# Eight gated blocks on one core: maxima without a clamp, a shared PSUM bank, one copy per mixture tile, and other orders

## The chip, the core and the metric

The kernel runs on one core of a Trainium2 chip. The core has five engines that work through their own lists in order and wait for each other by semaphores: TensorE (PE, with its weight loads PEld), VectorE (DVE), ScalarE (ACT), GpSimd (POOL) and SyncE (SP), which here only issues DMAs. TensorE writes to PSUM alone: 8 banks of 512 float32 per partition. The metric is the device time of one execution in microseconds; the time of a kernel is the median of its runs.

## The reference

`x` is (16, 112, 256), the context (16, 375, 256). Four layers follow each other, each an attention over the context and a feed-forward part, both gated:

```python
x = x + tanh(g_xattn[0]) * L0_xattn(layernorm(x), ctx, ...)          # 16 heads of 16
x = x + tanh(g_ffn[0])   * L0_ffn(layernorm(x), ...)                 # 8 experts, top 2
x = x + tanh(g_xattn[1]) * L1_xattn(layernorm(x), ctx, ctx, mask, ...)
x = x + tanh(g_ffn[1])   * L1_ffn(layernorm(x), ...)                 # 8 experts, top 2
x = x + tanh(g_xattn[2]) * L2_xattn(ctx, ctx, layernorm(x), ...)
x = x + tanh(g_ffn[2])   * L2_ffn(layernorm(x), ...)                 # tokens split over experts
x = x + tanh(g_xattn[3]) * L3_xattn(layernorm(x), ctx, ctx, mask, ...)  # one head
x = x + tanh(g_ffn[3])   * L3_ffn(layernorm(x), ...)                 # products of FP4-rounded values
```

The attention of layer 1 clips and masks its scores:

```python
scores = clip(q @ k.T * scale, -100.0, 100.0)
scores = where(mask == 0, -inf, scores)
out = softmax(scores) @ v
```

A mixture picks two of eight experts per token:

```python
expert_out = einsum('bsd,edo->bseo', x, expert_w) + expert_b
out = sum over the two chosen experts of gate * expert_out
```

## The kernel before

The 16 sequences (`b`) form four groups (`g`) of four; `x` stays in SBUF. The order of the work on PE, ACT, DVE and POOL is the order of the Python code: inside `tc.manual_schedule` nothing is reordered, so each engine meets its instructions as the lines are run.

**PSUM.** `wide` tiles (two banks each, three of them) and `bank` tiles (one bank, two of them) fill it. A new tile of a kind reuses an old one of that kind, and the first writer waits until the old one's readers are done.

**Layers 0 and 2** (`unmasked`) run per sequence: scores for the maxima (`maxima`, four steps `cp`, two wide tiles each, reduced on DVE, L455), the maxima split into three bf16 parts and transposed (`max_parts`, `max_rows`), transposed scores with the maximum subtracted by a small product (`exponentials`, L490 and L502, two wide tiles, ACT's exponential L511), the product with the values (`weighted`, L526, into the bank `po`), `normalised` on DVE, and `output` (L563). Keys of the sequence after next (`both_keys`, wide), values of the next (`values_of`, single banks) and the queries of the next group stand between.

**Layer 1** (`with_mask`) runs in 64 units, four per sequence. A unit issues the scores of the unit ahead (`masked_scores`: PE L439, then on DVE one operation that applies -100 and the upper bound with the mask, L589), transposes the exponentials of its own unit in two halves (`turned`, L623, copied by ACT or DVE, L627), multiplies those of the unit before with the values (`weighted_masked`, L640, into `po`), then `unit_rest`, and `masked_weights` of the unit ahead: DVE's maximum per half (L606), POOL's clamp of it to at most 100 (L608), ACT's four exponentials with their sums (L611). The inverse sums are spread on POOL (`one_over`, L655), transposed into a bank `pr` (`one_over_T`, L663), copied by ACT (L665); `normalised_masked` multiplies `po` with them on DVE, POOL adds a bias (`plus_bv`), and `output` multiplies with `wo` into a bank `py`, which ACT scales (L569) and POOL adds to `x` (L570). `mask_of` makes the upper bound on POOL (L580, L581).

**Mixtures.** `fill()`, called between the steps of the attention, advances three generators by one step each: `route` (norm, logits, top two, places in a table, indirect copies of the rows to DRAM), `products` (14 slots of 128 rows of one expert per group: L1127 and L1137 on PE, L1139 on ACT, L1142 on DVE, then a store) and `combine` (indirect gathers, L1157, and two additions each, L1165). A slot's product lies in one half of a wide tile, and the transposed rows of the next slot in the other half; ACT copies the rows, DVE adds the expert's bias, which a DMA has broadcast to 128 partitions. Group 0 of layer 0 begins to route at sequence 5 of layer 0; groups 2 and 3 are worked off in layer 1, those of layer 1 from its fifth sequence on into layer 2.

Of the kernel before, what the change touches and what calls it, by code (L numbers as in the profile page):

```python
# [25 lines left out]
E = 8  # L26
FF = 1024
FI = 704
P = 128
# [18 lines left out]
def tile_gated_xattn_stack(ctx: ExitStack, tc: tile.TileContext, a: dict, out: bass.AP):  # L48
# [4 lines left out]
    moe = ctx.enter_context(tc.tile_pool(name="moe", bufs=2))  # L53
# [18 lines left out]
    ctxT = [ctxp.tile([P, 2, T], F32, tag=f"ctx{b}", name=f"ctx{b}") for b in range(B)]  # L72
# [4 lines left out]
    def load_ctx(b):  # L77
        nc.sync.dma_start(ctxT[b], a["ctx"][:, :, b * T : (b + 1) * T])
# [38 lines left out]
    slot_rows = ramp(1, NS, P, "slot_rows")  # L117
    coef = const.tile([E, 2], F32, tag="coef", name="coef")
# [109 lines left out]
    def project(ps, w, c, rhs, n):  # L228

        for k in range(2):  # L230
            nc.tensor.matmul(  # L231
                ps[:, :n], w[:, k, c * P : (c + 1) * P], rhs[:, k, :], start=(k == 0), stop=(k == 1)
            )
# [22 lines left out]
    def attention(pool, layer, w):  # L256
# [7 lines left out]
        masked = layer == 1  # L264
        more = {}
# [81 lines left out]
        def keys_of(b, c):  # L347
            if b >= B:
                return
            if c == 0:  # L350
                kTs[b] = pool.tile([P, 2, T], F32, tag="kT", name=f"kT_{L}_{b}", bufs=3)
            pk = bank(f"pk_{L}_{b}_{c}")
            project(pk, w["wk"], c, rhs_of(b), T)
            if "bk" in w:
                nc.scalar.activation(kTs[b][:, c, :], pk[:, :T], AF.Identity, bias=w["bk"][:, c : c + 1])
            else:
                nc.scalar.copy(kTs[b][:, c, :], pk[:, :T])

        def both_keys(b):
            if b >= B:  # L360
                return
            kT = kTs[b] = pool.tile([P, 2, T], F32, tag="kT", name=f"kT_{L}_{b}", bufs=3)
            pk = wide(f"pk_{L}_{b}")
            for c in range(2):
                project(pk[:, c, :], w["wk"], c, rhs_of(b), T)
            if "bk" in w:
                for c in range(2):
                    nc.scalar.activation(kT[:, c, :], pk[:, c, :T], AF.Identity, bias=w["bk"][:, c : c + 1])
            else:
                nc.scalar.copy(kT, pk[:, :, :T])  # L370
# [58 lines left out]
        def scores(b, cp):  # L429
# [4 lines left out]
            for h in range(2):  # L434
                ps = wide(f"ps_{L}_{b}_{cp}_{h}")
                for i in range(2):
# [3 lines left out]
                        ps[:S, i, :T],  # L440
                        qms[g][rows, c, p, j * S : (j + 1) * S],
                        kTs[b][rows, c, :],
# [113 lines left out]
        def output(b):  # L556
# [4 lines left out]
            py = bank(f"py_{L}_{b}")  # L561
            for c in range(2):
                nc.tensor.matmul(py[:S, :D], oT[:, c, :], w["wo"][:, c, :], start=(c == 0), stop=(c == 1))  # L563
            if not masked:
                xb = x[g][:, j, :]
                nc.vector.scalar_tensor_tensor(xb, py[:S, :D], gate[:S, layer : layer + 1], xb, ALU.mult, ALU.add)
                return
            y = pool.tile([S, D], F32, tag="y", name=f"y_{L}_{b}", bufs=1)
# [4 lines left out]
        def mask_of(b):  # L573
# [5 lines left out]
            uppers[b] = pool.tile([S, T], F32, tag="upper", name=f"up_{L}_{b}")  # L579
            nc.gpsimd.tensor_scalar(uppers[b], mk, 0, -BIG, ALU.is_equal, ALU.mult)  # L580
            nc.gpsimd.tensor_scalar(uppers[b], uppers[b], 100.0, None, ALU.add)  # L581
            rss[b] = small.tile([S, H], F32, tag="rs", name=f"rs_{L}_{b}")

        def masked_scores(b, cp):
            if b >= B:
                return
            sm = exs[b, cp] = pool.tile([S, 4, T], F32, tag="ex", name=f"sm_{L}_{b}_{cp}", bufs=4)
            for h, ps in enumerate(scores(b, cp)):
                nc.vector.scalar_tensor_tensor(  # L589
                    sm[:, 2 * h : 2 * h + 2, :],  # L590
                    ps[:S, :, :T],
                    -100.0,
                    uppers[b][:, None, :].to_broadcast([S, 2, T]),
# [4 lines left out]
        def masked_weights(b, cp):  # L598
# [5 lines left out]
            for h in range(2):  # L604
                part = nmax[:, 2 * h : 2 * h + 2]
                nc.vector.tensor_reduce(part, sm[:, 2 * h : 2 * h + 2, :], AX.X, ALU.max, negate=True)  # L606

                nc.gpsimd.tensor_scalar(part, part, 100.0, None, ALU.min)  # L608
                for i in range(2 * h, 2 * h + 2):
                    head = 8 * c + 2 * i + p  # L610
                    nc.scalar.activation(  # L611
                        sm[:, i, :], sm[:, i, :], AF.Exp, bias=nmax[:, i : i + 1], accum_out=rss[b][:, head : head + 1]
# [18 lines left out]
        def weighted_masked(b, cp):  # L631
# [3 lines left out]
            if cp == 0:  # L635
                pos[b] = bank(f"po_{L}_{b}")
# [20 lines left out]
        def one_over_T(b):  # L657
            if b < 0:
                return
            rxf = rss.pop((b, "x")).rearrange("s h d -> s (h d)")  # L660
            pr = bank(f"pr_{L}_{b}")
# [27 lines left out]
        def unmasked(nxt, block):  # L689
# [12 lines left out]
            for b in range(B):  # L702
# [53 lines left out]
                fill()  # L756
                maxima(b + 2, 0)
                weighted(b, 1)
# [5 lines left out]
                values_of(b + 1, (2,))()  # L764
                if at == 1:
                    both_queries(g)
                maxima(b + 2, 1)
                fill()
# [10 lines left out]
        def unit_rest(b, cp, nxt):  # L779
# [3 lines left out]
            if cp == 0:  # L783
                one_over_T(b - 1)
                later.append(values_of(b + 1, (0, 1)))
            elif cp == 1:
                output(b - 1)
# [5 lines left out]
            if at == 3 and cp in (0, 1):  # L793
                queries_T(g, cp)
            elif at == 3 and cp == 2:
                for c in range(2):
                    queries(g, c)
            return later

        def with_mask(nxt):  # L800
# [8 lines left out]
            for u, (b, cp) in enumerate(units):  # L809
# [7 lines left out]
                fill()  # L817
                turned(b, cp, 0)
                if u:
                    weighted_masked(*units[u - 1])  # L820
                if cp % 2:
# [10 lines left out]
                elif cp == 3:  # L832
                    one_over(b)
# [15 lines left out]
            output(B - 1)  # L849
# [63 lines left out]
    )  # L913
    gate_weights = {}
# [9 lines left out]
    def mixture_weights(layer):  # L924
        L = f"L{layer}_ffn_"
        gate_weights[layer] = load(wpool, L + "gate_w", [P, 2, E], "gw"), load_row(L + "gate_b", "gb", E)

    def route(layer, g, out):
# [23 lines left out]
        xT = act.tile([P, 2, GS], F32, tag="xT", name=f"xT_{nm}")  # L952
        for k in range(2):
            pt = bank(f"pt_{nm}_{k}")
            for j in range(G):
                nc.tensor.transpose(pt[:, j * S : (j + 1) * S], xn[:, j, k * P : (k + 1) * P], ident[:S, :S])
            nc.scalar.copy(xT[:, k, :], pt[:, :GS])
            yield
        pl = bank(f"pl_{nm}")
# [46 lines left out]
        yield  # L1006


        pp = bank(f"pp_{nm}")
# [50 lines left out]
        pe = bank(f"pends_{nm}")  # L1060
# [6 lines left out]
        copy_out(0, 0)  # L1067
        yield
        pt = bank(f"ptab_{nm}")
# [8 lines left out]
        copy_out(0, 1)  # L1078
        yield
        for j in range(1, G):  # L1080
            for i in range(2):
                copy_out(j, i)
                yield

    def products(layer, g, routed):
# [13 lines left out]
        def weights_of(s):  # L1099
# [3 lines left out]
            w = ws[s] = moe.tile([P, 3 * D], F32, tag="w", name=f"w_{nm}_{s}", bufs=WB)  # L1103
            nc.sync.dma_start(
# [709 lines left out]
```

## Time and profile before

Nine runs: median 1622.64 us, 1616.84 to 1628.10. The profiled execution took 1616.01 us; its span, from the first instruction to the last, is 1614.2 us, at a mean granted TensorE clock of 0.973.

Stages of the span, busy us of each engine in them (all from the trace; "PE stands" is the length less PE's busy time):

| stage | us | length | PE | PE stands | DVE | ACT | POOL | clock |
|---|---|---|---|---|---|---|---|---|
| start | 0 to 23 | 23.0 | 13.1 | 9.9 | 2.1 | 4.2 | 12.0 | 0.90 |
| layer 0 attention, first mixtures | 23 to 393 | 370.0 | 340.1 | 29.9 | 223.6 | 150.8 | 89.7 | 0.95 |
| layer 1, masked attention, mixtures | 393 to 892 | 499.0 | 431.3 | 67.7 | 357.5 | 281.5 | 225.0 | 0.97 |
| layer 2 attention, last mixtures | 892 to 1250 | 358.0 | 339.9 | 18.1 | 207.6 | 159.2 | 93.6 | 0.99 |
| expert block of layer 2 | 1250 to 1370 | 120.0 | 116.6 | 3.4 | 49.6 | 42.9 | 46.1 | 1.00 |
| last layer | 1370 to 1614.2 | 244.2 | 223.2 | 21.0 | 164.5 | 112.2 | 84.0 | 0.99 |

A busy time counts an engine's instructions, not its waits for them; matmuls overlap, so PE's busy time is an upper bound of its work. The costliest groups that the change touches: L439 PE 1536 records of 531 ns; L589 DVE 128 of 929 ns; L606 DVE 128 of 923 ns; L611 ACT 256 of 600 ns; L608 POOL 128 of 221 ns; L1127 PE 448 of 403 ns; L1139 ACT 104 of 366 ns; L1142 DVE 112 of 423 ns. Views of waits name who waited, then (after the arrow) what ended the wait; a timeline shows the start, the length, the engine, the line and the shape, and in brackets how long the engine had stood before.

### The profile page before, as it was taken

How to read it: one execution, taken by the hardware profiler on the slowest of the kernel's cores; microseconds unless marked ns; L12 is line 12 of the kernel's file. 1: busy time of each engine (PE TensorE's matmuls, PEld its weight loads, DVE VectorE, ACT ScalarE, POOL GpSimd, SP SyncE). 2: the span in 40 equal slices, each digit the busy share in tenths (PEclk: the TensorE clock that was granted, in tenths of full speed). 3: DMA queues.
4: the chain of work that ended last, by engine and by line, in shares of the span. 5: the costliest groups of instructions: out<-in, count | busy, mean ns of one | idle time of the engine just before them, and what ended most of it. 6: DMA issues, size and time to landing. Idle time of an engine off the chain costs nothing.

```text
span 1614.2 us, 34976 instructions
## 1 busy us (share of the span) xinstructions
PE 1464.2 (91%) x13404; PEld 1015.7 (63%) x13404; DVE 1004.9 (62%) x1965; ACT 750.8 (47%) x1550; POOL 550.5 (34%) x1067
## 2 busy tenths in 40 slices
PE   6989899999888798897896899999999999899997
PEld 3555556666666566575674566666666888667765
DVE  2556555676767586777677365656566434476875
ACT  1444334344545555665654344444445333455532
POOL 3212122243444426427317214223212343242342
PEclk8889999999999999999998899999999999999999
DMA  8671014344434243441441242531002551100000
GB/s 245 212 258 49 2 36 120 117 124 108 121 109 127 86 131 108 123 121 60 125 126 56 81 115 71 156 104 32 8 2 86 164 176 49 38 16 19 16 9 18
DMA packets 127262, 150.37 MB, mean 93 GB/s; under 512 B 13496, under 2 KB 118328, under 8 KB 125048
## 3 DMA queue, kind: packets, MB, share of 16 engines
q1 hardware_dynamic: 120520, 133.45, 27.6%
q0 software_dynamic: 6144, 14.69, 3.1%
q8 instruction: 106, 1.74, 0.4%
q14 instruction: 60, 0.49, 0.1%
q10 hardware_dynamic: 432, 0.01, 0.0%
HBM read 103.80 MB, written 44.30 MB: 92 GB/s over the span
## 4 chain that ended last, share of the span: by engine, by line
PE 69%; DVE 14%; ACT 9%; POOL 3%; issue 3%; DMA 1%; SPq 0%; POOLq 0%; ACTq 0%; DVEq 0%
PE pv L406 8%; PE ps L439 8%; PE pk L231 7%; PE pm_m L1127 6%; PE pt L490 5%; PE po L526 4%; PE pe L623 4%; PE py_f L1285 3%; PE ph L1269 3%; PE py L563 3%; PE pq L231 3%; PE pgu_h L1615 2%; DVE nm L455 2%; ACT sm L611 2%; PE py L1649 2%
## 5 line engine op out<-in xcount | busy, mean ns | idle before, releaser
L455 DVE TENSOR_REDUCE nm<-ps 112x2 f32<-112x750 f32 x256 | 228.0, 932 | 188.6 <-PE ps L439 188.2
L439 PE MATMUL ps<-kT,qm 32*112 32x375 f32 x1536 | 196.4, 531 | 19.2 <-ACT kT L370 7.7
L511 ACT ACTIVATE ex<-pt 125x896 f32<-125x896 f32 x192 | 165.6, 914 | 68.9 <-PE pt L502 68.0
L611 ACT ACTIVATE sm<-sm,nmax 112x375 f32<-112x375 f32 x256 | 152.4, 600 | 27.0 <-POOL nmax L608 27.0
L589 DVE SCALAR_TENSOR_TENSOR sm<-ps,up 112x750 f32<-112x750 f32 x128 | 113.5, 929 | 64.5 <-PE ps L439 60.8
L623 PE MATMUL pe<-ident,sm 112*125 112x112 f32 x768 | 118.1, 287 | 37.4 <-ACT sm L611 30.6
L623 PEld LDWEIGHTS pe<-ident,sm 112*125 112x125 f32 x768 | 104.3, 196 | 68.8 <-ACT sm L611 58.2
L1127 PE MATMUL pm_m<-w_m,xgT_m 128*128 128x256 f32 x448 | 125.8, 403 | 7.6 <-DVE nm L455 4.8
L439 PEld LDWEIGHTS ps<-kT,qm 32*112 32x112 f32 x1536 | 66.5, 173 | 79.5 <-issue 27.1
L406 PE MATMUL pv<-w_L_xattn_wv,ctx 128*125 128x256 f32 x384 | 101.1, 401 | 16.0 <-ACT y L569 7.9
L606 DVE TENSOR_REDUCE nmax<-sm 112x2 f32<-112x750 f32 x128 | 112.9, 923 | 0.0
L490 PE MATMUL pt<-qm,kT 32*125 32x224 f32 x1536 | 109.3, 379 | 1.1 <-DVE nm L455 0.7
L1127 PEld LDWEIGHTS pm_m<-w_m,xgT_m 128*128 128x128 f32 x448 | 76.8, 190 | 43.7 <-ACT eT L627 14.9
L1142 DVE TENSOR_TENSOR y_m<-pm_m,w_m 128x256 f32<-128x256 f32 x112 | 47.3, 423 | 84.9 <-ACT xgT_m L1139 78.8
L627 ACT COPY eT<-pe 125x672 f32<-125x672 f32 x96 | 68.8, 717 | 62.2 <-PE pe L623 59.8
L231 PE MATMUL pk<-ctx,w_L_xattn_wk 128*128 128x375 f32 x256 | 93.5, 498 | 1.8 <-ACT qm L392 0.9
L526 PE MATMUL po<-ex,vpad 125*32 125x112 f32 x3072 | 94.6, 263 | 0.3 <-ACT ex L511 0.3
L406 PEld LDWEIGHTS pv<-w_L_xattn_wv,ctx 128*125 128x125 f32 x384 | 68.7, 191 | 40.9 <-ACT y L569 13.7
L427 POOL TENSOR_SCALAR oT<-oT,w_L_xattn_bv 128x112 f32<-128x112 f32 x64 | 35.8, 569 | 168.5 <-DVE oT L553 112.9
L526 PEld LDWEIGHTS po<-ex,vpad 125*32 125x32 f32 x3072 | 71.0, 110 | 34.0 <-issue 27.2
L490 PEld LDWEIGHTS pt<-qm,kT 32*125 32x125 f32 x1536 | 72.2, 184 | 25.1 <-issue 14.9
L1139 ACT COPY xgT_m<-pm_m 128x256 f32<-128x256 f32 x104 | 38.1, 366 | 103.5 <-PE pm_m L1137 103.2
(311 smaller groups left out, 2820.6 us busy)
## 6 DMA issues: line engine op xcount, KB each, us to landing
w_m<-in_L_ffn_expert_w_dram SPq DMA_DIRECT2D x112, 256.0 KB
w<-in_L_ffn_w_dram SPq DMA_DIRECT2D x16, 1024.0 KB
xg_m<-rows_in SPq DMA_DIRECT2D x112, 128.0 KB
w_m<-in_L_ffn_expert_b_dram SPq DMA_DIRECT2D x112, 128.0 KB
rows_out<-y_m SPq DMA_DIRECT2D x112, 128.0 KB
rows_in<-zero SPq DMA_DIRECT2D x2, 4992.0 KB
rows_out<-zero SPq DMA_DIRECT2D x2, 4992.0 KB
ctx<-in_ctx_dram SPq DMA_DIRECT2D x16, 375.0 KB
```

What stands on the lines that cost most here:

```text
L231: nc.tensor.matmul(ps[:, :n], w[:, k, c * P : (c + 1) * P], rhs[:, k, :], start=(k == 0), stop=(k == 1))
L406: nc.tensor.matmul(pv[:TC, i * D : (i + 1) * D], rhs_of(b)[:, k, t * TC : (t + 1) * TC], w["wv"][:, k, :], start=(k == 0), stop=(k == 1),)
L439: nc.tensor.matmul(ps[:S, i, :T], qms[g][rows, c, p, j * S : (j + 1) * S], kTs[b][rows, c, :], start=True, stop=True,)
L455: nc.vector.tensor_reduce(nms[b][:, cp, 2 * h : 2 * h + 2], ps[:S, :, :T], AX.X, ALU.max, negate=True)
L490: nc.tensor.matmul(pairs[r // 2][:TC, r % 2, q * 2 * S : (q + 1) * 2 * S], kTs[b][rows, c, t * TC : (t + 1) * TC], qms[g][rows, c, :, j * ...
L511: nc.scalar.activation(e[:, 2 * h : 2 * h + 2].rearrange("t r q p s -> t r (q p s)"), pairs[h][:TC, :, : 4 * S], AF.Exp)
L526: nc.tensor.matmul(po[32 * r : 32 * r + 32, (2 * c + p) * S : (2 * c + p + 1) * S], vp[:, t, 4 * c + r, p : p + 2, :], e[:, r, q, p, :], s ...
L589: nc.vector.scalar_tensor_tensor(sm[:, 2 * h : 2 * h + 2, :], ps[:S, :, :T], -100.0, uppers[b][:, None, :].to_broadcast([S, 2, T]), ALU.ma ...
L606: nc.vector.tensor_reduce(part, sm[:, 2 * h : 2 * h + 2, :], AX.X, ALU.max, negate=True)
L611: nc.scalar.activation(sm[:, i, :], sm[:, i, :], AF.Exp, bias=nmax[:, i : i + 1], accum_out=rss[b][:, head : head + 1])
L623: nc.tensor.transpose(pt[:TC, i, t * S : (t + 1) * S], sm[:, 2 * h + i, t * TC : (t + 1) * TC], ident[:S, :S])
L1127: nc.tensor.matmul(pt[:, 1, :D], xgT[:, k * P : (k + 1) * P], w[:, k * D : (k + 1) * D], start=(k == 0), stop=(k == 1),)
```

## The change

- **No clamp.** The context tiles get a 376th column of zeros, so the masked layer's keys get a 376th column, and the upper bound there is -100. Scores, maxima and keys of layer 1 run over 376 columns; the maximum is then at least -100, and POOL's clamp goes. The exponentials still run over 375.
- **One bank.** `output(b - 1)` allocates the bank of `po` of sequence b and puts its product into columns 256 on; the inverse sums are transposed into columns 224 on of their own `po`. `output` is split: the product stands ahead of `weighted_masked`, ACT's scaling (`output_added`) behind it. `one_over` moves to the start of the fourth unit, `one_over_T` behind `weighted_masked`.
- **Queries of layer 1** use wide tiles, both halves at once (`both_queries_T`, `both_queries`).
- **Mixtures.** A third product per slot (three rows of ones times the bias as three bf16 parts) adds the bias on PE; one ACT copy takes the slot's product and the next slot's transposed rows together. The parts are made once per layer and kept in DRAM, three rows per expert; a slot loads its three rows.
- **Routing** uses wide tiles, has other steps between its parts (17 instead of 18), and issues the indirect copies two at a time at the end.
- **Order in `unmasked`.** `weighted(b, 1)` stands ahead of `maxima(b + 2, 0)`, and `values_of(b + 1, (2,))` behind `maxima(b + 2, 1)`. `weights_down` has one more step.
- The pool `moe` is opened beside the attention's pool and closed with it.

```diff
-    ctxT = [ctxp.tile([P, 2, T], F32, tag=f"ctx{b}", name=f"ctx{b}") for b in range(B)]
+    ctxZ = [ctxp.tile([P, 2, T + 1], F32, tag=f"ctx{b}", name=f"ctx{b}") for b in range(B)]
+    ctxT = [t[:, :, :T] for t in ctxZ]
...
     def load_ctx(b):
+        nc.gpsimd.memset(ctxZ[b][:, :, T:], 0.0)
...
+        TK = T + 1 if masked else T
...
             oT = oTs.pop(b)
-            py = bank(f"py_{L}_{b}")
+            if masked and b + 1 < B:
+                pos[b + 1] = bank(f"po_{L}_{b + 1}")
+                py = pos[b + 1][:, 2 * P :]
+            else:
+                py = bank(f"py_{L}_{b}")
...
+            return py
+
+        def output_added(b, py):
...
             y = pool.tile([S, D], F32, tag="y", name=f"y_{L}_{b}", bufs=1)
             nc.scalar.mul(y, py[:S, :D], gate[:S, layer : layer + 1])
...
+            up = uppers[b] = pool.tile([S, T + 1], F32, tag="upper", name=f"up_{L}_{b}")
+            nc.gpsimd.memset(up[:, T:], -100.0)
...
                 nc.vector.tensor_reduce(part, sm[:, 2 * h : 2 * h + 2, :], AX.X, ALU.max, negate=True)
-
-                nc.gpsimd.tensor_scalar(part, part, 100.0, None, ALU.min)
...
-            if cp == 0:
+            if (b, cp) == (0, 0):
                 pos[b] = bank(f"po_{L}_{b}")
...
-            pr = bank(f"pr_{L}_{b}")
+            pr = pos[b][:, 2 * S :]
...
+                weighted(b, 1)
                 maxima(b + 2, 0)
-                weighted(b, 1)
...
-                values_of(b + 1, (2,))()
                 if at == 1:
                     both_queries(g)
                 maxima(b + 2, 1)
+                values_of(b + 1, (2,))()
...
-            if at == 3 and cp in (0, 1):
-                queries_T(g, cp)
+            if at == 3 and cp == 0:
+                both_queries_T(g)
             elif at == 3 and cp == 2:
-                for c in range(2):
-                    queries(g, c)
+                both_queries(g)
...
+                if cp == 3:
+                    one_over(b)
                 turned(b, cp, 0)
+                py = output(b - 1) if cp == 1 else None
                 if u:
                     weighted_masked(*units[u - 1])
+                if cp == 0:
+                    one_over_T(b - 1)
+                if py is not None:
+                    output_added(b - 1, py)
...
     def mixture_weights(layer):
...
+        rest = moe.tile([P, 2 * D], F32, tag="w", name=f"eb_{layer}", bufs=WB)[:E, :D]
+        nc.sync.dma_start(rest, a[L + "expert_b"])
+        parts = moe.tile([P, 4, D], BF16, tag="xy", name=f"bparts_{layer}", bufs=3)[:E, :3, :]
+        for i in range(3):
+            nc.gpsimd.tensor_copy(parts[:, i, :], rest)
+            if i < 2:
+                nc.gpsimd.tensor_tensor(rest, rest, parts[:, i, :], ALU.subtract)
+        nc.sync.dma_start(bias_rows[layer].rearrange("(e i) d -> e i d", i=3), parts)
...
+        yield
+        pt = wide(f"pt_{nm}")
         for k in range(2):
-            pt = bank(f"pt_{nm}_{k}")
             for j in range(G):
...
-        pp = bank(f"pp_{nm}")
+        yield
+        pp = wide(f"pp_{nm}")[:, 0, :]
...
-            nc.sync.dma_start(w[:, 2 * D :], a[L + "expert_b"][bass.ds(e, 1), :].partition_broadcast(P))
+            bp = moe.tile([3, D], BF16, tag="bp", name=f"bp_{nm}_{s}", bufs=WB)
+            nc.sync.dma_start(bp, bias_rows[layer][bass.ds(e * 3, 3), :])
...
-                        stop=(k == 1),
+                        stop=False,
                     )
+                nc.tensor.matmul(pt[:, 1, :D], ones3, bp, start=False, stop=True)
...
-                xgT = turnedT[s + 1] = moe.tile([P, D], F32, tag="xgT", name=f"xgT_{nm}_{s + 1}")
-                nc.scalar.copy(xgT, pt[:, 0, :D])
+            xy = moe.tile([P, 2, D], F32, tag="xy", name=f"xy_{nm}_{s}", bufs=3)
+            nc.scalar.copy(xy[:, lo : 1 + hi, :], pt[:, lo : 1 + hi, :D])
+            turnedT[s + 1] = xy[:, 0, :]
             if s >= 0:
-                y = moe.tile([P, D], F32, tag="y", name=f"y_{nm}_{s}")
-                nc.vector.tensor_tensor(y, pt[:, 1, :D], w[:, 2 * D :], ALU.add)
-                stores.append((s, y))
+                stores.append((s, xy[:, 1, :]))
```

## The prediction

> **What bounds the kernel now.** I read the page's first rows and its chain first, then the stage table above, then the waits of PE stage by stage, then the timeline of the longest ones.
>
> ```profile
> PE 1464.2 (91%) x13404; PEld 1015.7 (63%) x13404; DVE 1004.9 (62%) x1965; ACT 750.8 (47%) x1550; POOL 550.5 (34%) x1067
> PE 69%; DVE 14%; ACT 9%; POOL 3%; issue 3%; DMA 1%; SPq 0%; POOLq 0%; ACTq 0%; DVEq 0%
> ```
>
> PE works through its list in order and is busy 91% of the span, so a change pays in two ways: less PE work, or fewer of the 150 us in which PE stands. The stage table says where these are: 68 us in the masked layer (393 to 892 us), 30 in layer 0, 18 in layer 2, 4 in the expert block, 21 in the last one. The waits of PE, 393 to 909 us (who waited <- for whom: total us, times, longest us):
>
> ```profile
> PE pe L623 <- ACT sm L611: 30.6, 24, 6.2
> PE pv L406 <- ACT y L569: 7.9, 14, 0.6
> PE pv L406 <- ACT rT L665: 7.4, 15, 0.7
> PE pt_a L323 <- DVE vpad L416: 5.2, 6, 1.5
> PE pe L623 <- DVE nmax L606: 4.4, 1, 4.4
> PE pq L231 <- ACT qm L338: 4.3, 3, 1.4
> PE pq L231 <- ACT kT L355: 2.0, 3, 0.7
> ```
>
> Rows two to four and six to seven (26.8 us) are waits for one of the two single banks, in which pr, py, pv, pk, pt_a and pq follow each other while po holds the other. Rows one and five (35 us) are the transposes waiting for exponentials. The timeline of the longest kind shows why:
>
> ```profile
> 449.86 0.93 POOL L1157 DMA_INDIRECT yg_m<-rows_out,index_m  x1 [0.30 <-issue]
> 450.82 0.97 POOL L570 TENSOR_TENSOR x<-x,y 112x256 f32<-112x256 f32 x1
> 451.88 0.46 POOL L608 TENSOR_SCALAR nmax<-nmax 112x2 f32<-112x2 f32 x2
> 452.20 0.61 ACT L611 ACTIVATE sm<-sm,nmax 112x375 f32<-112x375 f32 x1 [4.15 <-POOL nmax L608]
> 452.95 1.60 PE L623 MATMUL pe<-ident,sm 112*125 112x112 f32 x6 [4.41 <-DVE nmax L606]
> ```
>
> The clamp takes POOL 0.2 us, but it stands in POOL's queue behind gathers and additions; ACT waits 4.15 us for it, PE 4.41. Such clusters lie near 452, 559 and 866 to 898 us. Each is followed by a stretch of half clock:
>
> ```profile
> 452.00:458.83 6.83, 5.88 (x37) 4.20 (x37) 1.76 (x3) 3.51 (x11) 6.15 (x9) 0.50 0.39 109
> 865.02:878.67 13.65, 9.83 (x80) 7.43 (x80) 8.61 (x13) 6.70 (x19) 11.49 (x20) 0.50 0.22 67
> ```
>
> (columns: length; busy us of PE, PEld, DVE, ACT, POOL; clock; DMA.) Five such stretches (452, 558, 865, 889, 899 us) hold 34.2 us of PE work, some 17 us too many at half speed.
>
> **The change, part by part** (minus is gain).
>
> *No clamp.* 128 POOL operations of 221 ns go, and with them a place in POOL's queue between DVE and ACT. PE's waits for exponentials over 0.8 us are 4.41, 3.52, 6.24, 1.97, 1.11, 2.85 and 1.69 in the clusters, and four of 1.1 to 1.6 elsewhere (26.8 in all). At 452 and 559 nothing else is late: DVE has the maxima at 448.75, so the first transposes could start near 449 and only the usual 0.6 stays: -6.7. At 866 to 898 the mask tile is late next: POOL builds it (L580, L581) at 861.7 to 864.5, behind the rows of the next norm, and the scores of batch 15 wait for it on DVE until 864.52. Of these 13.9 us I take 60%: -8.3. The four others mostly stand behind qm copies: 0. Half clock: the first two stretches go (11.5 us of work, -5.7); of the other three (22.7 us, worth 11.3) I take half, -5.7. Sum -26.4; bounds 0 and -43.9 (26.8 + 17.1). The 376th column costs 752 instead of 750 elements in 128 rows of 929 ns, 0.3 us of DVE in all.
>
> *One bank for po, pr and py.* pr goes into po's own bank, py into the next batch's. PE's waits for y and rT (15.3) are then gone, as the next allocation is two steps old: -14.5, bounds -15.3 and -7 (if ACT's queue paces the units instead). Two waits move: py now stands ahead of weighted, so oT must be ready 0.7 us sooner (around 817 us oT is there at 818.97 and py would come at 820.3: covered by pm and pe; 0 there, up to 1 us a batch without mixture work), and the reciprocal at the start of the fourth unit makes DVE wait for the last exponentials, some 0.4 us off the path.
> What would speak against it: the Trainium skill (PSUM — Partial Sum Buffer, "PSUM bank collisions raise a hardware error") says that two engines must not touch one bank at once, even at other addresses, so y's read and weighted's writes must be kept apart. No row before shows such a pair. Where y came first, PE would stand for each of 15 reads (0.44 us to start and 0.47 to run by the row of y): +14, and the gain of this part would be gone. The changed order issues y behind weighted, so ACT would be the one that waits; y's reader is an addition on POOL that nobody needs soon.
>
> *Queries in wide tiles.* The 11.5 us of pt_a and pq waits (three groups) go but for 1.5: -10, bounds -11.5 and -5 (the four qm copies, 0.72 us each, still stand before the exponentials).
>
> *Mixtures: one copy, bias on PE.* 112 slots: 22 in layer 0, 62 in the masked layer, 28 in layer 2. DVE loses 47.3 us (112 x 423 ns). ACT's copy grows from 366 ns (256 wide) to some 580 (between 525 at 448 and 717 at 672): +22 us on an engine busy 56% of the masked stage; hidden behind PE in dense units (PE 28.7 of 30 us at 800 to 830), 2 us paid there where the next product is close. The tile is given back by this copy alone, no longer by a DVE operation queued behind 1.8 us reductions. PE gains a product of 3 x 256 in bf16 per slot; no row has it. Nearest: four bf16 records of 112 columns take 0.30 us until the next work starts (1166.45 to 1166.75), 0.075 each, 0.17 by width; four float32 records of 256 columns (each product is recorded twice) take 0.88 until the next line starts (811.14 to 812.02), 0.22 each. A part of the 0.075 does not grow with the width, so 0.135. PE is the bound wherever mixtures run, so +15.1 (8.4 masked, 6.7 elsewhere), bounds +8.4 and +24.6. The bias broadcast (128 KB a slot) becomes 1.5 KB; nothing waits for it in these rows: 0. SP issues as many DMAs a slot; the store into bias_rows holds SP's list until POOL has split the biases (six casts and four subtractions in all, under 1 us each), twice; weights and rows are fetched two or three slots ahead, each some 5 us: 0, or 5 us if not.
>
> *Routing.* It moves to wide tiles, with a step between what DVE prepares and what PE reads. Waits for single banks and for routing's DVE work are 3.8 us in the masked stage (table, pends, cnt, keepb), 6.1 in layer 0, and 2.2 for the split weights of wd: -8, bounds -12 and +10 (some 40 more wide tiles in a ring of three).
>
> *Order in layers 0 and 2.* The waits there:
>
> ```profile
> PE ps L439 <- ACT kT L370: 7.7, 9, 0.9
> PE ps L439 <- ACT kT L368: 6.0, 9, 0.7
> ```
>
> weighted(b,1), 0.9 us, now fills these 13.7 us. But it used to stand between the scores and the next transposed scores, whose second half reuses the tile of the first maxima. Where these scores start at 1164.71, the first maximum ends at 1166.54; without weighted, PE would be there at 1166.04 (0.83 for the scores, 0.30 for L475, 0.2 for the first half): 0.5 us back in each of 18 places. -13.7 + 9 = -4.7, bounds -13.7 and 0.
> values(2) moves behind maxima(b+2,1). Of three wide tiles the exponentials hold two, so the second half of these scores waits for the first exponential. Before, values covered that exactly: behind L502 at 1167.91 came pv, then ps at 1168.97, just as the exponential ended (1168.07 + 0.87). Now the first half runs 0.4 us, PE stands about 0.5, then comes the second half, then pv. 22 batches (the three of a group's queries are covered by pq): +11, bounds 0 and +15.
>
> *Start, expert block, last block:* the 16 memsets lie in POOL's idle 4.5 to 12 us; the pool that moved changes only which old tiles the last block's overlie: 0.
>
> Sum: masked -26.4 - 14.5 - 10 - 3 + 8.4 + 2 = -43.5; layers 0 and 2: -5 - 4.7 + 11 + 6.7 = +8. Total -35.5 on the profiled run's own 1616.0: 1580.5. The median of the runs lies 6.6 above that run, so 1587.
>
> **Rivals.** *More of it:* the second halves do not wait, all gaps and half clocks go. Masked -43.5 - 11.3 (5.6 of gaps, 5.7 of clock), unmasked -5 - 13.7 + 6.7 = -12: -67, 1556. For it: the regular kT waits; against it: the tile ring and the late mask.
> *The wait moves:* in the clusters the mask tile and DVE's additions take the clamp's place (8 us instead of 26), ACT's longer queue gives back half of the bank waits and of the queries'. -8 - 7 - 5 - 3 + 10.4 + 8 = -5: 1618. For it: ACT's 5 us of exponentials and copies a unit of 6.7 to 7.4; against it: ACT waited for POOL, not POOL for ACT.
> *Slower: the ring of three wide tiles.* Routing, two-sided scores and queries all draw from it; in 28 batches of layers 0 and 2 PE would stand at both halves and at routing. None of the gains there (5 of routing, 4.7 of order) is then had, and the masked 43.5 are eaten from 1.3 us a batch on (28 x 1.3 + 6.7 = 43); at 2 us (62.7) the sum is +19, 1642. For it: the exponential that ends exactly when the tile is asked for; against it: PE waits for wide tiles there less than 10 us in a layer now.
> That sharing does nothing is no case: PE has no wait left between py and weighted in the changed order.
>
> **How the numbers follow.** Forecast (gain of 18 to 52) 0.58, more of it 0.18, the wait moves 0.14, the ring 0.10. About 0.3% (5 us) is what runs of this kernel can tell. Faster: 0.58 + 0.18 + half of the third, 0.83; same 0.06; slower 0.11. The range leaves out the ring and the far half of "more": 1552 to 1624.
>
> **What would show it.** The masked stage shorter by about 43 us; no waits of pv for y or rT; no gap over 3 us before pe and no half clock at 452 and 558; pq without gaps. Layers 0 and 2 unchanged or longer by 8 us, with new waits of ps for ex of some 0.5 us. Bias products 0.1 to 0.2 us apart. Wrong if layers 0 and 2 get longer by 20 us or more, if the clusters stay, or if a bias product costs PE more than 0.25 us.

## The result, and the profile after

The changed kernel takes 1634.99 us (median of 10 runs, 1628.62 to 1637.51) where the kernel before takes 1623.32 beside it (31 runs): a ratio of 1.0067, 95% interval 1.005 to 1.0085. It is slower by 0.7%, outside the forecast range of 1552 to 1624. Its profiled execution took 1636.23 us, 20 more than that of before, with a span of 1634.5; that of before was the fastest of all its runs, and by the medians the difference is 12 us.

The first row of the page of the changed kernel (busy us of each engine, share, instructions):

```profile
PE 1521.6 (93%) x13516; PEld 1027.3 (63%) x13516; DVE 967.7 (59%) x1853; ACT 776.3 (47%) x1547; POOL 530.5 (32%) x982
```

PE stands for 1634.5 - 1521.6 = 113 us, before for 150: the waits fell by 37 us. PE's busy time rose by 57 us. Stage by stage, between the same reductions on DVE in both traces:

| stage | before | after | half clock before | after |
|---|---|---|---|---|
| layer 0, first to last maximum | 341.6 | 351.3 | 34.1 | 41.0 |
| layer 1, first to last maximum | 484.8 | 476.5 | 27.9 | 41.0 |
| from there to the first full sequence of layer 2 | 25.1 | 19.4 | 13.1 | 0 |
| layer 2, to its last maximum | 315.2 | 337.5 | 0 | 13.7 |
| whole span | 1614.2 | 1634.5 | 87 | 110 |

PE's waits in the masked layer of the changed kernel (403 to 924 us; who waited <- for whom: total us, times, longest):

```profile
PE pe L636 <- ACT sm L624: 15.1, 19, 2.7
PE pe L636 <- DVE sm L604: 11.3, 7, 3.7
PE po L570 <- POOL oT L429: 4.6, 2, 3.9
PE pm_m L1160 <- DVE sm L604: 3.6, 5, 0.9
PE ps L441 <- ACT qm L394: 3.4, 6, 1.0
```

All waits of pv, pt_a for vpad and pq are gone from the head of this list, and the 30.6 us of pe for exponentials are 15.1; what is new is the second row, pe behind DVE, and the third, output's product behind POOL's bias addition. In layers 0 and 2 the waits of ps for kT (13.7 us) are gone as well, and the whole trace has this in their place (before it was 2.5 us, 6 times):

```profile
PE ps L441 <- ACT ex L513: 12.4, 28, 0.7
```

The groups of a mixture slot (busy us, mean ns of one; products, bias product, copy), and one slot with what follows it on PE, first before, then after:

```profile
L1160 PE MATMUL pm_m<-w_m,xy_m 128*128 128x256 f32 x416 | 116.6, 403 | 9.8 <-DVE sm L604 3.6 <-DVE nm L457 2.8 <-DMA w_m<-in_L_ffn_expert_w_dram 1.0
...
L1173 ACT COPY xy_m<-pm_m 128x512 f32<-128x512 f32 x112 | 63.2, 565 | 131.6 <-PE pm_m L1171 74.3 <-issue 34.8 <-PE pm_m L1167 3.7
...
L1167 PE MATMUL pm_m<-bp_m,ones 3*128 3x256 bf16 x112 | 31.2, 279 | 0.0
```

```profile
594.68 1.13 PE L1127 MATMUL pm_m<-w_m,xgT_m 128*128 128x256 f32 x4
595.64 0.38 PE L1137 MATMUL pm_m<-ident,xg_m 128*128 128x128 f32 x2
595.86 1.43 PE L231 MATMUL pk<-ctx,w_L_xattn_wk 128*128 128x375 f32 x4
```

```profile
559.93 1.13 PE L1160 MATMUL pm_m<-w_m,xy_m 128*128 128x256 f32 x4
561.00 0.28 PE L1167 MATMUL pm_m<-bp_m,ones 3*128 3x256 bf16 x1
561.21 0.44 PE L1171 MATMUL pm_m<-ident,xg_m 128*128 128x128 f32 x2
561.48 1.43 PE L235 MATMUL pk<-ctx,w_L_xattn_wk 128*128 128x376 f32 x4
```

From the first product to the next work are 1.18 us before and 1.55 us after. Over all full slots at full clock the median is 1546 ns, before 1186: the bias product costs PE 0.36 us a slot. Only 0.21 of it lies between its own start and the transposes'; 0.10 is a later start behind the products, 0.05 lies between the two transposes.

A long gap of before is left, at 566 us:

```profile
564.64 0.48 DVE L1198 SCALAR_TENSOR_TENSOR x<-yg_m,picks_m,x 112x256 f32<-112x256 f32 x1 [3.74 <-DMA yg_m<-rows_out,index_m]
...
565.73 1.43 DVE L1198 SCALAR_TENSOR_TENSOR x<-yg_m,picks_m,x 112x256 f32<-112x256 f32 x1 [0.60 <-DMA yg_m<-rows_out,index_m]
...
567.08 1.77 DVE L621 TENSOR_REDUCE nmax<-sm 112x2 f32<-112x752 f32 x2
...
568.04 0.61 ACT L624 ACTIVATE sm<-sm,nmax 112x375 f32<-112x375 f32 x1 [3.67 <-DVE nmax L621]
...
569.84 1.57 PE L636 MATMUL pe<-ident,sm 112*125 112x112 f32 x6 [3.71 <-DVE sm L604]
```

POOL's gathers used to hold the clamp. Now DVE itself stands 3.74 us for a gather, with the next maxima queued behind the addition that needs it; ACT and PE wait as long as before. At 882 us POOL's queue delays another operation as it had delayed the clamp:

```profile
881.63 1.36 POOL L429 TENSOR_SCALAR oT<-oT,w_L_xattn_bv 128x112 f32<-128x112 f32 x2
882.28 2.05 PE L570 MATMUL po<-w_L_xattn_wo,oT 128*112 128x256 f32 x4 [3.87 <-POOL oT L429]
```

DVE had written oT by 875.84, but the bias addition L429 stands behind two indirect copies and two gathers on POOL, and output's product, which now comes earlier, stands 3.87 us for it. Here are three of the stretches at half clock (length; busy us of PE, PEld, DVE, ACT, POOL; clock; DMA):

```profile
568.50:575.30 6.80, 5.46 (x38) 4.49 (x39) 4.61 (x7) 3.54 (x11) 0.00 (x0) 0.50 0.24 71
...
1118.00:1124.80 6.80, 6.80 (x64) 4.33 (x63) 2.16 (x4) 1.41 (x3) 0.93 (x1) 0.50 0.07 19
104.20:111.00 6.80, 6.80 (x62) 4.35 (x64) 3.38 (x5) 1.96 (x4) 3.70 (x6) 0.50 0.01 4
```

The first follows the gap above. The two others follow no gap of 2 us at all; PE is busy throughout them, at half speed.

### The profile page after: what moved, and what is told of

Its sections match the earlier page's. It is cut to its first block, busy times and chain, and to the rows that moved or that the text cites. A ratio compares the mean times of both kernels' runs of the same rounds, so it can differ in the third digit from the quotient of the medians.

```text
span 1634.5 us, 34973 instructions
## 1 busy us (share of the span) xinstructions
PE 1521.6 (93%) x13516; PEld 1027.3 (63%) x13516; DVE 967.7 (59%) x1853; ACT 776.3 (47%) x1547; POOL 530.5 (32%) x982
## 4 chain that ended last, share of the span: by engine, by line
PE 49%; DVE 7%; ACT 4%; POOL 4%; issue 2%; SPq 1%; DMA 0%; POOLq 0%; ACTq 0%; DVEq 0%
PE ps L441 5%; PE pm_m L1160 4%; PE pv L408 4%; PE pk L235 4%; PE py_f L1318 3%; PE ph L1302 3%; PE pe L636 3%; PE pt L492 3%; PE pgu_h L1649 2%; PE po L528 2%; PE py L1683 2%; PE po L653 2%; PE pm_m L1171 1%; PE pq L235 1%; PE pz L1580 1%
## 5 line engine op out<-in xcount | busy, mean ns | idle before, releaser
L441 PE MATMUL ps<-kT,qm 32*112 32x375 f32 (+1 forms) x1536 | 219.1, 534 | 19.6 <-ACT ex L513 12.4
L604 DVE SCALAR_TENSOR_TENSOR sm<-ps,up 112x752 f32<-112x752 f32 x128 | 114.4, 933 | 79.5 <-PE ps L441 73.5
L636 PE MATMUL pe<-ident,sm 112*125 112x112 f32 x768 | 115.6, 285 | 26.5 <-ACT sm L624 15.1
L1173 ACT COPY xy_m<-pm_m 128x512 f32<-128x512 f32 x112 | 63.2, 565 | 131.6 <-PE pm_m L1171 74.3
L1160 PE MATMUL pm_m<-w_m,xy_m 128*128 128x256 f32 x416 | 116.6, 403 | 9.8 <-DVE sm L604 3.6
L441 PEld LDWEIGHTS ps<-kT,qm 32*112 32x112 f32 x1536 | 73.0, 173 | 78.9 <-ACT ex L513 32.0
L492 PE MATMUL pt<-qm,kT 32*125 32x224 f32 x1536 | 117.0, 387 | 4.0 <-DVE nm L457 2.6
L429 POOL TENSOR_SCALAR oT<-oT,w_L_xattn_bv 128x112 f32<-128x112 f32 x64 | 35.9, 569 | 254.1 <-DVE oT L555 156.2
L621 DVE TENSOR_REDUCE nmax<-sm 112x2 f32<-112x752 f32 x128 | 113.0, 924 | 0.0
L1160 PEld LDWEIGHTS pm_m<-w_m,xy_m 128*128 128x128 f32 x416 | 72.0, 190 | 49.1 <-ACT eT L640 16.2
L235 PE MATMUL pk<-ctx,w_L_xattn_wk 128*128 128x376 f32 (+1 forms) x256 | 91.7, 492 | 0.9 <-ACT qm L394 0.9
L528 PEld LDWEIGHTS po<-ex,vpad 125*32 125x32 f32 x3072 | 73.9, 113 | 27.9 <-issue 21.3
L418 ACT COPY vpad<-pv 125x256 f32<-125x256 f32 x96 | 32.7, 375 | 99.1 <-PE pv L408 99.1
```

Source lines behind the costliest of these rows:

```text
L235: nc.tensor.matmul(ps[:, :n], w[:, k, c * P : (c + 1) * P], rhs[:, k, :n], start=(k == 0), stop=(k == 1))
L441: nc.tensor.matmul(ps[:S, i, :TK], qms[g][rows, c, p, j * S : (j + 1) * S], kTs[b][rows, c, :TK], start=True, stop=True,)
L492: nc.tensor.matmul(pairs[r // 2][:TC, r % 2, q * 2 * S : (q + 1) * 2 * S], kTs[b][rows, c, t * TC : (t + 1) * TC], qms[g][rows, c, :, j * ...
L528: nc.tensor.matmul(po[32 * r : 32 * r + 32, (2 * c + p) * S : (2 * c + p + 1) * S], vp[:, t, 4 * c + r, p : p + 2, :], e[:, r, q, p, :], s ...
L604: nc.vector.scalar_tensor_tensor(sm[:, 2 * h : 2 * h + 2, :], ps[:S, :, :TK], -100.0, uppers[b][:, None, :].to_broadcast([S, 2, TK]), ALU.max,
L636: nc.tensor.transpose(pt[:TC, i, t * S : (t + 1) * S], sm[:, 2 * h + i, t * TC : (t + 1) * TC], ident[:S, :S])
```

## The experiments

In the runs of this section the kernel before takes 1676 to 1684 us, not 1623 (the last section shows what differs). They were made on three chips; that of the first runs is not recorded. So every kernel is compared with the runs of before beside it, by the ratio; us are worked out on 1676.

**The changed kernel and the kernel before, again** (no edit).

> The changed kernel again, since the kernel before took 1678 us in the last four runs and 1623 beside the first one. Theory A: the ratio belongs to the kernels, 1.007 again, whatever the kernel before takes. Theory B: the gain depends on the granted clock, since the kernel before has more of its work in stretches of half clock there; where the kernel before takes 1678, the changed kernel takes 1659 + 5 = 1664 (the run with the old order plus the 5 us between the two runs with old slots), a ratio of 0.992.

> The kernel before, profiled beside the others. If it takes 1678 again, its trace shows where the 55 us lie. Theory B: in stretches of half clock, 55 us more work in them than in the first trace (89 us), and nearly all in layer 0 and the masked layer. Theory C: in transfers that land later, so that PE stands 55 us more at the same clock.

c1_before 1675.27 us; c1_after 1667.81, a ratio of 0.9965 (0.9941 to 0.9989): here the change gains 6 us. Which of the two kernels is faster is not a matter of the kernels alone; theory B's direction is right, its size (14 us) is not. The granted clock of each run gives its length at half clock, 2 x (1 - clock) x span: for the changed kernel 104 us in the mean of the first runs and 148 here, for the kernel before 87 in the one first run that has it and 150 here. Half of the 19 us between these rises is over half of the 17 us between the two ratios. The trace of c1_before divides its extra 53 us between theories B and C, about half each (last section).

**What the bias product costs.** e2_no_bias (first diff) and e6_bias_first (second), both from the changed kernel:

```diff
                     nc.tensor.matmul(
...
-                        stop=False,
+                        stop=(k == 1),
                     )
-                nc.tensor.matmul(pt[:, 1, :D], ones3, bp, start=False, stop=True)
```

```diff
+                nc.tensor.matmul(pt[:, 1, :D], ones3, bp, start=True, stop=False)
                 for k in range(2):
...
-                nc.tensor.matmul(pt[:, 1, :D], ones3, bp, start=False, stop=True)
```

> The third product of each slot is left out (the expert biases are missing from the output). Theory A: 112 slots by 0.36 us, 1595 us; in the trace the time from a slot's second product to its transposes falls by 0.2 us or more. Theory B: 112 by 0.135 us, 1620 us. Theory C (PE has slack around the slots, so what the product takes is given back as waits): within 5 us of the changed kernel, 1630 to 1640.

> The bias product stands ahead of the slot's two products and not behind them; its inputs come from DMAs, so it doesn't wait for the copy. Theory A1 (the product costs 0.28 us of PE wherever it stands): within 4 us of the changed kernel. Theory A2 (it costs so much because it follows float32 products and the transposes follow it, so PE drains between the types): still two changes of type, the same. Theory A3 (behind the second product PE has to stand, ahead of the first one it fills a wait for the copied rows): 10 to 25 us less than the changed kernel.

e2: 0.9749 (0.9711 to 0.9787), 36 us below the changed kernel: theory A, and the slot is back at 1186 ns. So the 40 us (112 x 0.36) lie on the path, within what these runs can tell; no slack around the slots shows. e6: 0.9887 (0.9845 to 0.9929), 1650 us against 1668. Its slot takes 1393 ns; 112 x 153 ns are 17 us. A slot with the same successor as the one above:

```profile
566.53 0.28 PE L1159 MATMUL pm_m<-bp_m,ones 3*128 3x256 bf16 x1
566.74 1.13 PE L1161 MATMUL pm_m<-w_m,xy_m 128*128 128x256 f32 x4
567.71 0.38 PE L1171 MATMUL pm_m<-ident,xg_m 128*128 128x128 f32 x2
567.93 1.43 PE L235 MATMUL pk<-ctx,w_L_xattn_wk 128*128 128x376 f32 x4
```

1.40 us against 1.55: the product's own 0.21 is left, the later starts around it are gone. The gain is that of A3, its reason isn't: no wait for rows is filled, since PE has no gap in either. Why the product costs 0.15 more behind the float32 products than ahead of them stays open; the number of changes of type is the same.

**Old slots, and slots alone.** e3_old_slots gives the changed kernel the slots of before, e11_slots_alone the kernel before the new ones; e8_one_copy_sbuf keeps the single copy and adds the bias on DVE behind it:

```diff
             nc.scalar.copy(xy[:, lo : 1 + hi, :], pt[:, lo : 1 + hi, :D])
+                nc.vector.tensor_tensor(xy[:, 1, :], xy[:, 1, :], w[:, 2 * D :], ALU.add)
```

> The slots as they were before (bias added on DVE, copy of 256 columns, broadcast of the bias), all else as in the changed kernel. Theory A: 1600 us (the 40 us come back, DVE's 47 us of additions cost some 5). Theory B: 1625 (the 15 us of PE come back, 5 are lost to DVE's queue and to the second reader of a tile). If the single copy was worth more than my 0, it shows as the difference to the kernel without the bias product.

> The kernel before with the new slots alone (one copy per tile, bias product on PE behind the slot's products). Theory A (PE pays 0.36 us a slot, 40 in all, and the single copy gives some of it back): 25 to 40 us slower than the kernel before, the same on any chip. My prediction's terms: 15 + 2, 17 us slower.

> The masked part alone, and in the slots one copy per tile as in the changed kernel, but the bias stays on DVE and is added behind the copy, in SBUF. PE does what it did before, and the tile is free when the copy is done. If the single copy is worth the 11 us that lie between the kernel with old slots and the one without the bias product: a ratio to before 0.007 below that of the masked part alone, 0.964 where that took 0.971. If those 11 us were only what DVE's additions cost: no gain against the masked part.

e3 0.9786 (0.9754 to 0.9819), 30 us below the changed kernel, theory A; e11 1.0157 (1.0133 to 1.0182), 26 us slower: PE's 40 less 14 that come back. e8 0.9715 (0.9675 to 0.9755), no better than the masked part alone: the single copy shows no gain (with two buffers of its tile, where the changed kernel has three). What comes back is then DVE's 47 us of additions or the bias broadcast that goes with them; no run tells these two apart.

**The masked part.** e5_masked_part is before with everything that the change does in layer 1's attention; e7_clamp_alone takes only the clamp out. (Both, and e11, also have the moved pool and the added step of `weights_down`.)

> The kernel before with the masked part of the change alone (no clamp, shared bank, wide queries, the order of the unit); routing, slots and the order in layers 0 and 2 as before. By my prediction 1622 less 26, 14.5 and 10: a ratio of 0.969. If the run with old slots and old order (0.976) owes its gain to the masked part, this is 0.976 to 0.981; if it owes it to the routing in wide tiles, 0.985 to 0.995.

> The kernel before with the clamp alone taken out (376th column, mask of -100 there); banks, queries, order of the unit as before. My prediction: 26 us less than the kernel before (0 to 44), half of it from stretches of half clock that go with the long gaps at 449, 555 and 861 us. Rival (the wait moves to the scores' mask step on DVE, and the half clock stays): 5 to 12 us less.

e5 0.9707 (0.9681 to 0.9732), 49 us faster, about as forecast (0.969); e7 0.9896 (0.9866 to 0.9926), 17 us, between the forecast and the rival. Bank, queries and order of the unit together are the other 32. At half clock e7 has 22 us less than the runs of before beside it (124 for 147), e5 36 less (114 for 150).

**The order in layers 0 and 2.** e1_order undoes it in the changed kernel, e12_order_alone does it in the kernel before, e13_weighted_alone does its first move only:

```diff
+                weighted(b, 1)
                 maxima(b + 2, 0)
-                weighted(b, 1)
```

> Theory A (the bias product on PE took the gain: some 0.36 us a slot, 40 us in all, where I had 15): the order in layers 0 and 2 is a side matter, the time falls by 3 to 10 us against the changed kernel, to about 1628. Theory B (the order in layers 0 and 2 took it: 1 us in every batch that has no mixture work and more where there is some): the time falls by 20 to 30 us, to about 1610.

> The kernel before with the new order in layers 0 and 2 alone. My prediction: 6 us slower (4.7 gained by the product with the values that stands in the wait for the keys, 11 lost at the second halves). From the runs so far (1668 with, 1659 without): 5 to 9 slower. If the new short waits also bring stretches of half clock in layers 0 and 2 where there were none: 10 to 20 slower.

> Of the new order, the move of the product with the values ahead of the first scores of the sequence after next alone; the values stay where they were. My prediction: 5 us faster than the kernel before (13.7 of waits for keys filled, 9 given back). If the waits for keys come back whole as waits for the first maximum: no difference.

e1 0.9881 (0.9851 to 0.9911), 14 us below the changed kernel, between the theories; e12 1.0053 (1.003 to 1.0076), 9 us slower; e13 0.9972 (0.9957 to 0.9988), 5 faster. So the move of the values costs 14. With the new order there is more half clock: e12 has 14 us more than before, c1_after 22 more than e1. A place of it in the changed kernel:

```profile
1116.88 0.48 PE L441 MATMUL ps<-kT,qm 32*112 32x375 f32 x2
1117.83 1.48 PE L441 MATMUL ps<-kT,qm 32*112 32x375 f32 x4 [0.47 <-ACT ex L513]
1119.24 1.22 PE L408 MATMUL pv<-w_L_xattn_wv,ctx 128*125 128x256 f32 x2
```

The second half of the scores waits 0.47 us for the first exponential, and the values, which used to fill this, come behind. The half clock of 1118 us begins just behind this wait.

**Routing.** e9_old_route undoes it in the changed kernel, e14_route_alone does it in the kernel before, e4_slots_order has masked part and routing only, e16_route_single is e4 with one indirect copy a step:

```diff
             for i in range(2):
                 copy_out(j, i)
-            yield
+                yield
```

> Old slots and the old order in layers 0 and 2 together; what is left of the change is the masked part and the routing. Both theories: about what I had forecast for these parts alone, 1622 less 52 to 60: 1565 to 1575. Theory D (the masked part and the routing bring far less than the 60 us that I gave them): 1595 to 1610.

> The changed kernel with the routing of before (single banks, its old steps, one indirect copy a step). My prediction took routing in wide tiles for a gain of 8 us: then this is 8 us slower than the changed kernel. The runs so far (with old slots and order, 1636 with the new routing and 1622 without) say that the routing costs 14: then this is 14 us faster, 1621 beside a kernel before of 1623, 1654 beside one of 1676.

> The kernel before with the new routing alone (wide tiles, new steps, indirect copies two at a time at the end). My prediction: 8 us faster (bounds 12 faster, 10 slower). The two pairs of runs so far say 14 slower (old slots, old order) and no difference (new slots, new order); if what differs there is the standing of ACT and DVE for something that the trace does not show, beside POOL's indirect copies, then this kernel's trace has 10 us or more of it over the kernel before's 49.

> The kernel with old slots and old order (masked part and new routing, a ratio of 0.976), but with one indirect copy a step at the routing's end, so that it has 19 steps, not 17. If the pairs of copies, which hold POOL's queue, are what the new routing costs in the masked layer: the ratio of the masked part alone, 0.971. If the wide tiles are, or where its steps fall among the units: 0.976 or more.

e4 0.976 (0.9727 to 0.9793), 9 us above e5; e14 1.008 (1.0057 to 1.0104), 13 slower than before; e9 0.996 (0.9939 to 0.998), no difference. In the traces the new routing lengthens the masked layer in all three pairs (500 to 526 us in e14, 459 to 476 in e4, 469 to 480 against e9) and shortens layer 2 in e9's pair alone (357 to 346). e14 has 46 us of unrecorded standing and not 59, so its expectation's reason falls. e16 0.9733 (0.9702 to 0.9764) lies between its two cases: the pairs of copies are not shown to be the cause. By the granted clock of the runs, half clock would make up most of the cost: e14 has 19 us more of it than before, e4 23 more than e5, worth some 9 and 12 us; in e9's pair, where the time does not differ, c1_after has 16 less. Which part of the routing brings it stays open.

**Bias first, with order and routing of before**, and **the parts that gain**:

> The masked part, one copy per tile with the bias product on PE ahead of the slot's products; order and routing as before. PE pays 0.21 us a slot, 23 us, DVE has no additions. Against the masked part alone: 23 less 11, 12 us slower, if the terms add up; equal to it if PE's slack in the slots takes up the rest.

> The masked part of the change and the one move that paid by itself (the product with the values ahead of the first scores); slots, routing and the place of the values as before. If the terms add up: 49 and 5 us less than the kernel before, a ratio of 0.968; if the move's gain came from where a stretch of half clock happened to fall: 0.971, that of the masked part alone.

e10 0.9794 (0.9762 to 0.9825), 15 us above e5, where the sum of terms was 12: they add up, PE shows no slack. e15 is the masked part with e13's move and nothing else of the change: 1622.95 us, 0.9637 (0.9606 to 0.9669), 61 us faster than before and the lowest ratio of all. The two gains by themselves come to 54; where the other 7 come from is open. It beats both kernels here; how much of it is had where the kernel before takes 1623 was not measured.

## Why the prediction was wrong

Alone on the kernel before, in us (half clock: mean length at half clock less that of the runs of before beside it, good to some 8 us; where PE is busy, half of it is lost):

| term | forecast | measured | half clock |
|---|---|---|---|
| no clamp | -26.4 | -17 (e7) | -22 |
| one bank and queries | -24.5 | -32 (e5 less e7) | -14 |
| slots (product, copy) | +17.1 | +26 (e11) | +2 |
| product with the values moved | -4.7 | -5 (e13) | +5 |
| values moved | +11 | +14 (e12 less e13) | +9 |
| routing | -8 | +13 (e14) | +19 |

The sum is -0.5 (-49.1 + 26.3 + 8.9 + 13.4); the whole change measured -5.9 beside the same runs. At half clock the parts come to -1 us, the whole change to -2.

In the first pair of traces the miss can be split by what PE does. Forecast 1580.5 for the profiled run, measured 1636.2: 55.7 us (48 by the medians, 1587 and 1635).

- **The sum of the waits was right, in part by luck.** The terms for waits alone (clamp -15, bank -14.5, queries -10, routing -8, order +6.3, copy +2) come to -39; PE stood 37 us less. The kinds were as described: no waits for y and rT, none for kT, new ones of some 0.5 us for ex. But pe's waits for exponentials fell by 8.6 us (35.0 to 26.4), not by 15, and output's product, put at 0, stands 4.6 us for oT. In layers 0 and 2, where +6.3 was forecast, the 13.7 us for kT gave way to 9.9 more for ex and some 2 more for maxima.
- **The bias product was mis-sized:** "so 0.135", where the median says 0.36: 40.3 us and not 15.1, 25 of the miss. The bound of 0.22 was passed too. The step that failed is the price by the nearest rows: they were records in a run of their own kind, and I costed the record's width, not the later starts of the work before and behind it. That all of it would lie on the path was right (e2).
- **The half clock was counted for the clamp alone:** "the first two stretches go", half of the others, -11.4. Instead the stretches grew from 87 to 110 us, 23 us more; if half is lost, +11.7: 23 of the miss, by one trace each (the changed kernel's runs have 85 to 121 us). By itself the term was about right: e7 has 22 us less, worth 11. The step that failed is that the order and the routing were given no half clock; alone they bring 14 and 19 us more of it. In the first pair this shows in two places, each about half of the 23. In layers 0 and 2 there are 20.6 us more: seven of the 28 short waits for ex are followed by half clock in the next slot of the clock's grid (last section), 37.5 us in all. In the masked layer and up to layer 2, where 23 us were to go, the 41 us of before stay 41: the stretch at 452 is gone, but the one at 558 is back at 568, since "nothing else is late" overlooked DVE's additions, which stand for the same gathers, and others go with new waits, as that for oT at 882.
- **Routing** has the wrong sign when measured alone ("-8", where e14 gives +13). In the first pair it can't be told apart: of the 7 us that remain there, 2 are waits (37 less for 39), 5 are PE work that I can't place.

Of the rivals, "the wait moves" names what happened at 566 us; the ring of three came near the time, but not by its mechanism: its waits for wide tiles appeared (ps for ex, 28 times), at 0.44 us each and not the 1.3 to 2 us a batch that it needed. The wrong signs were named beforehand and appeared: clusters that stay, a product above 0.25 us, layers 0 and 2 longer by 32.

## What to carry to other kernels

Cost an added matrix product by the time from the work before it to the work behind it, in a slot of the same kind, and try it at both ends of the slot: here its place decided 0.15 of 0.36 us. Moving work from an engine with gaps to the one that is 91% busy cost about its full length here (36 of 40 us), so the engine relieved must have been on the path by as much. Taking one operation out of a queue that holds gathers leaves the next one there to wait (the bias addition at 882 us). Of a change with several parts, run each alone: here two parts gain 61 us together (e15), the others give nearly all of it back.

## What the runs showed of the hardware

**The clock.** The granted clock changes on a grid of 3.41 us. Over the 20 traces, from 34 us on, a slot of this grid at full clock was followed by half clock by how long PE stood in it: under 1 us 45 times in 8,059; 1 to 1.5 us 73 in 331; 1.5 to 2 us 139 in 190; over 2 us 107 in 107. In the first 34 us it was 12 in 39 of those with over 2 us. So the standing of PE within a slot does not decide alone: in the changed kernel's trace seven of the 27 slots with a wait for ex were followed by half clock, though PE stood only 0.6 to 1.0 us in them. A stretch then lasts 3.4 us or a few times that, so that two waits of 0.5 to 0.8 us in one slot can cost as much again or more. The Trainium skill (TensorE: Matmul & The Clock Gate, "What's actually happening") has half clock come after at least one idle window of about 3.4 us; here, from 34 us on, 2 us of standing within a slot sufficed each time.

**Standing that no row explains.** Where the kernel before took 1668 (its profiled span), its trace has 49 us in which ACT or DVE stand for something not recorded ("remote"), and none in the trace of 1614. All ten lie beside POOL's indirect copies. One of them:

```profile
347.05 0.98 POOL L1157 DMA_INDIRECT yg_m<-rows_out,index_m  x1 [0.30 <-issue]
348.33 0.94 POOL L1157 DMA_INDIRECT yg_m<-rows_out,index_m  x1 [0.31 <-issue]
...
350.81 0.93 POOL L1157 DMA_INDIRECT yg_m<-rows_out,index_m  x1 [0.30 <-issue]
...
352.49 0.53 ACT L479 COPY mr<-pm 128x448 bf16<-128x448 bf16 x1 [8.17 <-remote]
...
353.07 1.22 PE L406 MATMUL pv<-w_wv,ctx 128*125 128x256 f32 x2 [4.13 <-issue]
```

ACT has stood 8.17 us, the last 6 of them with its input there (pm, which PE starts at 346.10 and has done by 346.5), and PE stands behind it. PE stands 173 us there and not 150, and 140 us are at half clock and not 87: 23 + 26 of the 53.5 us between the two traces of the kernel before. The changed kernel has 56 us of such standing there, the masked part alone 30, e4 82: the differences between kernels in the experiments contain it. Two of the ten end within 1 us of the landing of a packet on an instruction queue; whether instructions are fetched late behind the copies was not tried, and the cause stays open.
